# GroupNorm's small products on GpSimd, and the queries' last bias halves behind the first exponentials

## The chip, the core and the metric

The kernel runs on one core of a Trainium2 chip. The metric is the device time of one execution in microseconds (us), the median of several runs. Five engines matter: TensorE (PE in the profile; its weight loads are PEld), VectorE (DVE), ScalarE (ACT), GpSimd (POOL) and the queue that issues the transfers (SP). Each takes its own instructions strictly in order, and they wait for each other by semaphores.

## What is computed

Two attention blocks follow each other, for each of 8 images of 512 channels and 1024 tokens, all in float32:

```python
# layer 0: 32 groups, 8 heads of 64 channels
h   = group_norm(x, gn_weight, gn_bias)
q, k, v = split(w_qkv @ h + b_qkv)                  # per head
a   = softmax((q * s) @ (k * s)) @ v,  s = 64**-0.25
x   = x + w_proj @ a + b_proj
# layer 1: 8 groups, one head of 512 channels
xn  = group_norm(x, gamma, beta)
x   = x + p_w @ (softmax(q1 @ k1 / sqrt(512)) @ v1) + p_b    # q1, k1, v1 from xn
```

A group norm becomes a scale and an offset for each channel: `rstd = (var + eps) ** -0.5`, `s = rstd * weight`, `b = bias - mean * s`. For 512 channels on 128 partitions that is four columns.

## The kernel before

**Products.** Nearly all the work is matrix products on TensorE. The 512 x 512 products are made by Winograd's form of Strassen's scheme, with seven products of half the size in place of eight (`wino`), and the keys and queries of images 1 to 7 apply the scheme twice (`conv2`). Image 0 has its queries and keys from `conv`, with one level.

**conv2.** It works in four `pair`s, numbered `s` = 0 to 3, that hold the outer products (1, 5), (2, 6), (7) and (3, 4). Each pair runs seven inner steps in the order 1, 6, 2, 5, 7, 3, 4. Three pairs of PSUM banks take the sums: bank a for the inner products 1 and 2, b for 6, 7 and 4, c for 5 and 3. ScalarE copies bank a to bank b in step 1 (line 477). In pairs 2 and 3 VectorE adds a bank to what was there before (line 439, in `add`), and TensorE may go on with a bank only when VectorE has read it: step 7 needs bank b after step 6's addition (`u_q`), step 3 needs bank c after step 5's (`c_q`), step 4 needs bank b after step 7's. Pair 2 also sends eight additions of 128x256 to GpSimd (`more`, line 444), which read and write the blocks that pair 3 reads and overwrites. Steps 3 and 4 of a pair, and what is in its list `final`, are put on `tail`, which the next pair runs after its own step 1 (`finish()`).

**The bias of the queries.** `biased_half(i, c)` (line 446) adds it in place with two ScalarE instructions of 128x512 (line 451): for the channel tiles 2i and 2i+1, and the token half c. Half (0, 0) is at the end of pair 1, (1, 1) at the end of pair 2, (0, 1) and (1, 0) at the end of pair 3. The last two thus come just ahead of the attention of that image; its call of `psum_pools` runs what is left on `tail`.

**Attention of layer 0** (`attention0`). Eight stretches for each image: four pairs of heads `hp`, two token halves `tb`. A stretch makes eight tiles of scores (`sc`, two matmuls each), lets ScalarE take the exponential of each (line 590, `e`), sums them on VectorE (lines 592 and 594), and then makes the product with the values (`av`). The tiles of scores rotate through three PSUM pools with one buffer each, so tile n+3 can't start before the exponential of tile n is done. The first stretch reads channel tile 0 and token half 0 of the queries; the second stretch is the first that needs a token half 1. The caller hands in `extra`, sixteen lists of small work: `extra[0]` is run after the first stretch's exponentials have been written down and ahead of its `av`.

**GroupNorm.** `group_mean` and `affine` are two small products with a few small instructions behind. In `affine` (line 123) VectorE reads the variance from PSUM (`ve`, line 126), GpSimd takes the power (`rstd`, line 128), and VectorE makes `s`, `ms` and `b` (lines 130, 132, 134), each of 128x4. There are sixteen of them in a run: two in the prologue, one in the keys of image 1, six behind pair 2 of the queries of images 1 to 6 (line 883, for the next image's layer 0), and seven in layer 1's scores (line 860). The queries of image 7 have none, since no image comes after. `apply` (line 140) uses `s` and `b` on ScalarE; except in the prologue that is a whole stage later.

**What sets the order.** Matmuls are pinned to the order in which the program writes them (`tc.keep_in_program_order`), and so are a few instructions of the other engines. The others are put into their engine's queue by a planner, from its own costs of the instructions and with the order of the program as their priority.

Of the kernel before, what the change touches and what calls it, by code (L numbers as in the profile page):

```python
# [11 lines left out]
AF = mybir.ActivationFunctionType  # L12
ALU = mybir.AluOpType
# [16 lines left out]
def two_attention_blocks_kernel(  # L30
# [8 lines left out]
    nc = tc.nc  # L39
# [26 lines left out]
    def matmul(*args, **kw):  # L66
        tc.keep_in_program_order(nc.tensor.matmul(*args, **kw))  # L67
# [4 lines left out]
    def pcols(name):  # L72
        i = 4 * PARAMS.index(name)
        return par[:, i : i + 4]
# [14 lines left out]
    class GroupNorm:  # L89
# [33 lines left out]
        def affine(self, ps):  # L123
            matmul(ps, gm[:, self.layer, :], self.dv, start=True, stop=True)
            ve = small.tile([P, KC], F32, tag="ve", name=f"ve_{self.uid}")
            nc.vector.tensor_scalar(ve, ps, EPS, None, ALU.add)  # L126
            rstd = small.tile([P, KC], F32, tag="rstd", name=f"rstd_{self.uid}")
            nc.gpsimd.tensor_tensor(rstd, ve, mhalf, ALU.pow)  # L128
            self.s = small.tile([P, KC], F32, tag="s", bufs=4, name=f"s_{self.uid}")
            nc.vector.tensor_mul(self.s, rstd, pcols(f"gn_w{self.layer}"))  # L130
            ms = small.tile([P, KC], F32, tag="ms", name=f"ms_{self.uid}")
            nc.vector.tensor_mul(ms, self.gmean, self.s)
            self.b = small.tile([P, KC], F32, tag="b", bufs=4, name=f"b_{self.uid}")
            nc.vector.tensor_sub(self.b, pcols(f"gn_b{self.layer}"), ms)

        def apply(self, engine, dst, src, c):
            s, b = self.s[:, c : c + 1], self.b[:, c : c + 1]
# [38 lines left out]
    def main_path(ctx):  # L176
# [14 lines left out]
        def acc_tile(name):  # L191
            return ps_acc.tile([P, HT], F32, tag="acc", name=name)
# [5 lines left out]
        def psum_pools(stage, bufs):  # L198
            finish()
            ps_stack.close()  # L200
            ps_pools[:] = [
                ps_stack.enter_context(
                    tc.tile_pool(name=f"ps_{stage}_{n}", bufs=bufs, space=bass.MemoryType.PSUM)
                ) for n in "abc"
            ]

        def load_x(b, c, what):
            t = big_tile(f"{what}_{b}_{c}")
            nc.sync.dma_start(t, x[b, c * P : (c + 1) * P, :])
            return t  # L210
# [12 lines left out]
        def finish():  # L223
            while tail:
                tail.pop(0)()
# [187 lines left out]
                steps.append(make)  # L413
            return f, steps

        def conv2(n, f, bias, name, hooks=()):

# [3 lines left out]
            hooks = list(hooks)  # L423
# [22 lines left out]
            def biased_half(i, c):  # L446
                if bias is not None:
                    for r in range(2):
                        oc = 2 * i + r
                        t = out[oc][:, ts(c, HT)]  # L450
                        nc.scalar.activation(t, t, AF.Identity, bias=bias[:, oc : oc + 1])

            def pair(s, products, y, x, final):
                w = weights2[s // 2][:, (0, 2, 0, 1)[s] :]
# [82 lines left out]
            pair(1, (2, 6), [(0, 0), (0, 1)], [(1, 0), (1, 0)], [load_weight, lambda: biased_half(0, 0)])  # L537
            weights2.append(weight_part((n, 1)))
            pair(2, (7,), [(1, 0)], [(0, 1)], [lambda: biased_half(1, 1)])
            pair(3, (3, 4), [(0, 1), (1, 0)], [(0, 1), (1, 0)], [load_weight, lambda: biased_half(0, 1), lambda: biased_half(1, 0)])  # L540
            return out


# [262 lines left out]
        v, q, k, norm0, later = prologue()  # L806
# [8 lines left out]
        def all_background():  # L815
            run_background(len(background))

        def begun(load, norm, b, what):

            t = [None] * KC  # L820

            def start(c):
                t[c] = load(b, c, what)

            return (
                t, [lambda c=c: start(c) for c in range(KC)],
                [lambda c=c: norm.apply(nc.scalar, t[c], t[c], c) for c in range(KC)],
            )

        def attention_steps(a, scaled, b):  # L830
            af, steps = image_factors(a, f"a_{b}")
            return af, [[], [scaled, lambda: background.extend(steps)]]
# [24 lines left out]
        def norm_hooks(norm, uid):  # L857
            return [
                [], [], [all_background], [lambda: norm.group_mean(acc_tile(f"gmean_{uid}")[:, :KC])],
                [lambda: norm.affine(acc_tile(f"gvar_{uid}")[:, :KC])],  # L860
            ]

        def values(b, h, hooks=()):

            hf, steps = image_factors(h, f"h0_{b}")
            background.extend(steps)
            inner, steps = inner_factors(hf, f"h0_{b}")
            background.extend(steps)
            norm = None
            if b + 1 < B:  # L870
                norm = GroupNorm(0, f"0_{b + 1}")
                for c in range(KC):
                    background.append(lambda c=c: norm.stats(c, load_x(b + 1, c, "ahead")))
            v = by_token(weight("v"), hf, f"v0_{b}", middle=(2, 5, 6, 7), hooks=hooks, back=4, after=[load_weight])
            return v, inner, norm

        def keys_and_queries(b, f, norm, hooks):

            k = conv2("k", f, None, f"k0_{b}", hooks)
            hooks = [[all_background], [], []]  # L880
            if norm:
                hooks[1].append(lambda: norm.group_mean(acc_tile(f"gmean_0_{b + 1}")[:, :KC]))
                hooks[2].append(lambda: norm.affine(acc_tile(f"gvar_0_{b + 1}")[:, :KC]))
            q = conv2("q", f, pcols("bq0"), f"q0_{b}", hooks)
            return q, k

        def layer1_scores(b, h, hooks):
            hf, steps = image_factors(h, f"h1_{b}")
            background.extend(steps)
            g = conv(  # L890
                weight("m"), hf, ubias, f"g1_{b}", middle=(2, 5, 6, 7), hooks=hooks, back=4,
                after=[load_weight, lambda: background.extend(gsteps)],
            )
            stiles = [pair_tile(f"sg{i}_{b}") for i in (1, 2, 4)]
            halves = lambda t: (t[:, :HT], t[:, HT:])
            gf, gsteps = left_sums(
                [halves(t) for t in g[:2]], [halves(t) for t in g[2:]],
                [lambda j, t=t: t[:, j, :] for t in stiles], nc.vector.tensor_add, nc.vector.tensor_sub,
            )
            return hf, gf  # L900
# [22 lines left out]
        for b in range(B):  # L923
            extra = [[] for _ in range(2 * 2 * KC)]
            for i, fs in enumerate(later):
                extra[i] += fs
            later = []
            h, loads, applies = [], [], []
            if b > 0:
                h, loads, applies = begun(load_again, norm1, b - 1, "h1")  # L930
            elif B > 1:
                h, loads, applies = begun(load_x, norm0, 1, "h0")
            for f in loads:
                f()
            for i, f in enumerate(applies):
                extra[2 * i + 3].append(f)
            psum_pools(f"attention_{b}", 1)
            a, scaled = attention0(b, q, k, v, extra)
            psum_pools(f"products_{b}", 2)
            xt = [load_x(b, c, "x") for c in range(KC)]  # L940
            af, ends = attention_steps(a, scaled, b)
            if b > 0:
                hf, gf = layer1_scores(b - 1, h, ends)
                norm1 = projection(b, af, xt)
                if b + 1 < B:
                    h, loads, applies = begun(load_x, norm0, b + 1, "h0")
                else:
                    h, loads, applies = begun(load_again, norm1, b, "h1")
                ahead = [loads, *([f] for f in applies)]
                layer1_rest(b - 1, hf, gf, norm_hooks(norm1, f"1_{b}"), ahead)  # L950
                if b + 1 < B:
                    v, f, norm0 = values(b + 1, h)
                    q, k = keys_and_queries(b + 1, f, norm0, ())
            elif B > 1:
                v, f, norm0 = values(1, h, ends)
                norm1 = projection(0, af, xt)
                q, k = keys_and_queries(1, f, norm0, norm_hooks(norm1, "1_0")[1:])
            else:
                for f in sum(ends, []):
                    f()  # L960
                all_background()
                norm1 = projection(0, af, xt)
                finish()
                for f in sum(norm_hooks(norm1, "1_0"), []):
                    f()
                h, loads, applies = begun(load_again, norm1, 0, "h1")
                for f in loads + applies:
                    f()
# [151 lines left out]
    with ExitStack() as main_ctx:  # L1120
        main_path(main_ctx)
# [45 lines left out]
```

## Time and profile before

| | |
|---|---|
| time, median of 3 runs | 2918.28 us (2915.02 to 2919.66) |
| span of the profiled execution | 2912.7 us |
| PE busy | 2891.4 us (99%) |
| DVE busy | 1940.7 us (67%) |
| ACT busy | 872.3 us (30%) |
| POOL busy | 463.0 us (16%) |
| granted TensorE clock | full in all slices |
| `q` bias, line 451 | 56 instructions, 721 ns in the middle |
| `rstd`, line 128 | 16 instructions, 1017 ns in the middle |
| `s`, line 130 | 16 instructions, 161 to 684 ns, behind 22.2 us of idle VectorE in all |

A row of the groups of instructions gives line, engine, operation, what is written and read (`out<-in`), the shapes, and the count, then the busy time and the mean of one in ns, then the idle time of the engine ahead of it and who ended it. A row of the waits reads: engine, tile and line that waited, whom it waited for, total us, times, longest us. The timeline gives start and duration in us; the same instructions in a row are merged. The page's matmul ends are modelled, so what TensorE loses is best read from the starts of its instructions.

### The profile page before, as it was taken

The numbers are of one execution on the slowest core, as the hardware profiler recorded it, in microseconds if no ns is written. First come the engines' busy times: TensorE is split into PE (matmuls) and PEld (weight loads), VectorE is DVE, ScalarE is ACT, GpSimd is POOL, SyncE is SP. The second block draws the span as 40 slices with busy tenths as digits, with TensorE's granted clock in tenths as the row PEclk, the third lists the DMA queues.
The fourth block names the chain that finished last, engine by engine and source line by source line (L and its number), as shares of the span: only waits on it lengthen the run. The fifth ranks groups of instructions, "written<-read, shape, count | busy, mean of one in ns | idle before, by whom it ended". The sixth has DMA issues, their size and how long they took to land.

```text
span 2912.7 us, 28999 instructions
## 1 busy us (share of the span) xinstructions
PE 2891.4 (99%) x10838; PEld 1495.4 (51%) x10838; DVE 1940.7 (67%) x2661; ACT 872.3 (30%) x1117; POOL 463.0 (16%) x477
## 2 busy tenths in 40 slices
PE   9999999999999999999999999999999999999999
PEld 5436534565345653457434574346733458334544
DVE  5488677566766568665776567866577665776555
ACT  1252451214512055121551115411164112631110
POOL 3023220032100312003210122102111031110000
PEclk9999999999999999999999999999999999999999
DMA  8433303223122231222212232122411223012201
GB/s 276 163 125 119 147 19 116 76 92 131 38 93 91 95 113 48 83 92 108 103 48 80 92 135 77 48 80 95 151 60 44 80 102 141 35 51 73 91 4 66
DMA packets 84186, 267.97 MB, mean 92 GB/s; under 512 B 10371, under 2 KB 29891, under 8 KB 75974
## 3 DMA queue, kind: packets, MB, share of 16 engines
q1 hardware_dynamic: 83622, 265.89, 25.2%
q8 instruction: 87, 1.43, 0.2%
q14 instruction: 61, 0.50, 0.1%
q10 hardware_dynamic: 416, 0.16, 0.0%
HBM read 216.30 MB, written 49.72 MB: 91 GB/s over the span
## 4 chain that ended last, share of the span: by engine, by line
PE 94%; DVE 2%; issue 1%; ACT 1%; POOL 1%; DMA 0%; SPq 0%; DVEq 0%; POOLq 0%; ACTq 0%
PE av L67 15%; PE sc L67 15%; PE psb_sc L67 6%; PE psb_av L67 6%; PE psa_av L67 4%; PE psa_sc L67 4%; PE psc_av L67 4%; PE psc_sc L67 4%; PE psb_z L67 3%; PE psb_p L67 3%; PE psb_g L67 3%; PE psb_v L67 3%; PE psb_k L67 3%; PE psc_z L67 2%; PE psa_z L67 2%; PE psc_p L67 2%
## 5 line engine op out<-in xcount | busy, mean ns | idle before, releaser
L594 DVE TENSOR_TENSOR sum<-sum,e 128x1024 f32<-128x1024 f32 x384 | 518.9, 1351 | 40.4 <-ACT e L590 0.5
L590 ACT ACTIVATE e<-sc 128x1024 f32<-128x1024 f32 x512 | 475.7, 1048 | 63.1 <-PE sc L67 63.1
L67 PE MATMUL sc<-q,k 64*128 64x512 f32 x2048 | 461.8, 598 | 1.1 <-ACT e L590 1.1
L67 PE MATMUL av<-e,v 128*64 128x512 f32 x2048 | 453.6, 595 | 0.0
L67 PEld LDWEIGHTS sc<-q,k 64*128 64x128 f32 x2048 | 188.1, 185 | 248.0 <-ACT e L590 124.0
L67 PEld LDWEIGHTS av<-e,v 128*64 128x64 f32 x2048 | 141.4, 137 | 304.3 <-issue 304.3
L557 POOL TENSOR_TENSOR all_recs<-all_recs,rc 128x256 f32<-128x256 f32 x72 | 64.6, 897 | 896.9 <-DVE rc L555 896.9
L555 DVE RECIPROCAL rc<-sums 128x256 f32<-128x256 f32 x72 | 126.4, 1756 | 88.0 <-PE sums L67 85.7
L611 POOL TENSOR_TENSOR a<-a,r 128x512 f32<-128x512 f32 x56 | 112.1, 2002 | 267.8 <-DMA r<-rows 258.3
L608 ACT COPY a<-av 128x512 f32<-128x512 f32 x64 | 37.5, 586 | 320.9 <-PE av L67 320.9
L642 ACT ACTIVATE e<-e 128x512 f32<-128x512 f32 x96 | 60.5, 630 | 232.6 <-DVE e L641 232.6
L592 DVE TENSOR_TENSOR sum<-e,e 128x1024 f32<-128x1024 f32 x64 | 78.4, 1226 | 66.3 <-ACT e L590 66.3
L67 PE MATMUL psa_sc<-g,h 128*128 128x512 f32 x256 | 115.7, 594 | 0.0
L67 PE MATMUL psa_av<-e,z 128*128 128x512 f32 x256 | 113.3, 595 | 0.0
L140 ACT ACTIVATE h<-h,b,s 128x1024 f32<-128x1024 f32 x62 | 78.6, 1270 | 58.1 <-DMA h<-in_x 46.6
L128 POOL TENSOR_TENSOR rstd<-ve,mhalf 128x4 f32<-128x4 f32 x16 | 16.3, 1018 | 499.9 <-DVE ve L126 499.9
L67 PE MATMUL psb_q<-inner_h,w_q 128*128 128x256 f32 x294 | 75.5, 385 | 6.5 <-DVE u_q L439 6.5
L67 PEld LDWEIGHTS psa_sc<-g,h 128*128 128x128 f32 x256 | 48.1, 190 | 57.9 <-issue 56.2
L67 PEld LDWEIGHTS psa_av<-e,z 128*128 128x128 f32 x256 | 48.0, 190 | 57.3 <-issue 55.4
L67 PE MATMUL psb_k<-inner_h,w_k 128*128 128x256 f32 x294 | 75.3, 383 | 0.0
L249 ACT COPY t_sc<-psa_sc 128x512 f32<-128x512 f32 x32 | 18.7, 586 | 181.7 <-DVE x L843 152.4
L444 POOL TENSOR_TENSOR k<-k,k 128x256 f32<-128x256 f32 x28 | 20.1, 727 | 291.1 <-DVE u_k L439 291.1
(304 smaller groups left out, 4582.9 us busy)
## 6 DMA issues: line engine op xcount, KB each, us to landing
x<-in_x SPq DMA_DIRECT2D x36, 512.0 KB
h<-in_x SPq DMA_DIRECT2D x32, 512.0 KB
r<-rows SPq DMA_DIRECT2D x128, 128.0 KB
spill<-x SPq DMA_DIRECT2D x32, 512.0 KB
h<-spill SPq DMA_DIRECT2D x32, 512.0 KB
x<-spill SPq DMA_DIRECT2D x32, 512.0 KB
out<-x SPq DMA_DIRECT2D x64, 256.0 KB
w_p<-sums_p SPq DMA_DIRECT2D x8, 1792.0 KB
```

Of the source, the lines that this page charges most:

```text
L67: tc.keep_in_program_order(nc.tensor.matmul(*args, **kw))
L140: tc.keep_in_program_order(nc.scalar.activation(dst, src, AF.Identity, bias=b, scale=s))
L249: nc.scalar.copy(t1[i], ps["a", i])
L444: nc.gpsimd.tensor_tensor(d, x, y, ALU.add)
L555: nc.vector.reciprocal(rc, sums)
L557: nc.gpsimd.tensor_tensor(all_recs, all_recs, rc, ALU.add)
L590: nc.scalar.activation(e, sc, AF.Exp, scale=(C // 8) ** -0.5)
L592: nc.vector.tensor_add(total, es[0], e)
L594: nc.vector.tensor_add(total, total, e)
L608: nc.scalar.copy(dst, av)
L611: nc.gpsimd.tensor_tensor(dst, dst, r, ALU.mult)
L642: nc.scalar.activation(dst, dst, AF.Exp, scale=scale)
```

## The change

Two edits, independent of each other.

The first one moves `s`, `ms` and `b` from VectorE to GpSimd, right behind the power that they wait for. VectorE then has no instruction in a norm that waits for GpSimd.

The second one takes the bias halves (0, 1) and (1, 0) of the queries off the end of pair 3 and gives them to the caller in a list, `late`, which is added to `extra[0]` of the attention. They are then queued on ScalarE behind the eight exponentials of the first stretch. All bias instructions of `conv2` are pinned to the program's order.

```diff
@@ affine
-            nc.vector.tensor_mul(self.s, rstd, pcols(f"gn_w{self.layer}"))
+            nc.gpsimd.tensor_tensor(self.s, rstd, pcols(f"gn_w{self.layer}"), ALU.mult)
             ms = small.tile([P, KC], F32, tag="ms", name=f"ms_{self.uid}")
-            nc.vector.tensor_mul(ms, self.gmean, self.s)
+            nc.gpsimd.tensor_tensor(ms, self.gmean, self.s, ALU.mult)
             self.b = small.tile([P, KC], F32, tag="b", bufs=4, name=f"b_{self.uid}")
-            nc.vector.tensor_sub(self.b, pcols(f"gn_b{self.layer}"), ms)
+            nc.gpsimd.tensor_tensor(self.b, pcols(f"gn_b{self.layer}"), ms, ALU.subtract)
@@ conv2
-        def conv2(n, f, bias, name, hooks=()):
+        def conv2(n, f, bias, name, hooks=(), late=None):
...
-                        nc.scalar.activation(t, t, AF.Identity, bias=bias[:, oc : oc + 1])
+                        tc.keep_in_program_order(nc.scalar.activation(t, t, AF.Identity, bias=bias[:, oc : oc + 1]))
...
-            pair(3, (3, 4), [(0, 1), (1, 0)], [(0, 1), (1, 0)], [load_weight, lambda: biased_half(0, 1), lambda: biased_half(1, 0)])
+            last = [lambda: biased_half(0, 1), lambda: biased_half(1, 0)]
+            if late is not None:
+                late += last
+                last = []
+            pair(3, (3, 4), [(0, 1), (1, 0)], [(0, 1), (1, 0)], [load_weight, *last])
@@ keys_and_queries
-            q = conv2("q", f, pcols("bq0"), f"q0_{b}", hooks)
-            return q, k
+            late = []
+            q = conv2("q", f, pcols("bq0"), f"q0_{b}", hooks, late=late)
+            return q, k, late
@@ main loop
+            if b > 0:
+                extra[0] += late
             psum_pools(f"attention_{b}", 1)
...
-                    q, k = keys_and_queries(b + 1, f, norm0, ())
+                    q, k, late = keys_and_queries(b + 1, f, norm0, ())
...
-                q, k = keys_and_queries(1, f, norm0, norm_hooks(norm1, "1_0")[1:])
+                q, k, late = keys_and_queries(1, f, norm0, norm_hooks(norm1, "1_0")[1:])
```

## The prediction

> **What bounds the kernel.** The page first. TensorE is busy for 2891.4 of 2912.7 us and carries 94% of the chain that ended last, so only what lets TensorE start sooner counts. The waits of TensorE name few partners.
>
> ```profile
> PE 2891.4 (99%) x10838; PEld 1495.4 (51%) x10838; DVE 1940.7 (67%) x2661; ACT 872.3 (30%) x1117; POOL 463.0 (16%) x477
> ...
> PE psb_q L67 <- DVE u_q L439: 6.5, 6, 1.1
> ...
> PE psc_q L67 <- DVE c_q L439: 1.2, 6, 0.2
> PE sc L67 <- ACT e L590: 1.1, 7, 0.2
> ```
>
> Six waits in the queries, as many as there are queries with a norm behind pair 2 (images 1 to 6), and seven at scores, as many as there are attentions behind a `conv2`. The ends of matmuls are modelled, so these totals are too small; I take lengths from start to start. The timeline of VectorE in image 1's queries, pair 2 into pair 3, shows the first wait's cause:
>
> ```profile
> 321.30 0.16 DVE L126 TENSOR_SCALAR ve<-gvar 128x4 f32<-128x4 f32 x1 [0.25 <-PE gvar L67]
> 321.38 0.41 DVE L439 TENSOR_TENSOR q<-psb_q,c_q 128x256 f32<-128x256 f32 x1
> 324.37 0.68 DVE L130 TENSOR_TENSOR s<-rstd,par 128x4 f32<-128x4 f32 x1 [2.58 <-POOL rstd L128]
> ...
> 325.37 0.42 DVE L439 TENSOR_TENSOR q<-psc_q,u_q 128x256 f32<-128x256 f32 x1
> 325.70 0.41 DVE L439 TENSOR_TENSOR q<-psb_q,q 128x256 f32<-128x256 f32 x1
> 326.03 0.74 DVE L439 TENSOR_TENSOR u_q<-psb_q,q 128x256 f32<-128x256 f32 x2
> ...
> 323.32 1.02 POOL L128 TENSOR_TENSOR rstd<-ve,mhalf 128x4 f32<-128x4 f32 x1
> 324.31 0.72 POOL L444 TENSOR_TENSOR q<-q 128x256 f32<-128x256 f32 x1
> ...
> 327.35 0.72 POOL L444 TENSOR_TENSOR q<-q 128x256 f32<-128x256 f32 x1
> ```
>
> VectorE stands still for 2.58 us ahead of `s`: the power waits in GpSimd's queue behind four `more` additions and starts at 323.32 though `ve` was there at 321.46. Behind `s` stand the two bank reads of pair 2's steps 3 and 4 and then `u_q`, for which TensorE waits. Image 7's queries have no norm and are the control. The busy times by stretch, from the first matmul of pair 2's step 3 to the first score:
>
> ```profile
> 322.07:330.08 8.01, 6.74 (x30) 4.89 (x28) 5.07 (x15) 2.32 (x4) 5.10 (x7) 1.00 0.72 296
> 2466.26:2472.79 6.53, 6.48 (x31) 4.96 (x29) 4.63 (x12) 2.32 (x4) 4.27 (x7) 1.00 0.90 375
> ```
>
> The first column after the stretch is its length: 8.01 us in image 1, 6.53 in image 7. The norm costs TensorE 1.48 us there.
>
> The second loss, in the same view: a first stretch of attention behind `conv2` (image 1), and the one after it. Then ScalarE's timeline at the start.
>
> ```profile
> 330.08:345.60 15.52, 15.37 (x74) 4.95 (x73) 9.33 (x9) 10.01 (x13) 0.00 (x0) 1.00 0.33 120
> 345.60:360.26 14.66, 14.66 (x78) 5.37 (x74) 11.86 (x9) 9.14 (x11) 2.24 (x2) 1.00 0.05 18
> ...
> 329.78 2.56 ACT L451 ACTIVATE q<-q,par 128x512 f32<-128x512 f32 x4 [0.95 <-DVE q L439]
> 332.24 1.00 ACT L590 ACTIVATE e<-sc 128x1024 f32<-128x1024 f32 x1
> ```
>
> The first stretch takes 15.52 us, a later one 14.66: 0.86 us lost. The four bias instructions hold ScalarE until 332.3, so the first exponential starts 2.16 us after the first score (330.08); in the next stretch it starts 1.17 us after (346.77 against 345.60). The fourth tile of scores needs that exponential's bank and starts at 333.30.
>
> **What the Trainium skill says.** "Perfetto Trace Analysis", Sequencer Loop: an engine instruction waits for its semaphores in its engine's queue; the 2.58 us ahead of `s`, with ready bank reads behind it, agree. "GPSIMD Engine Reference", 3.1: a tensor_tensor of 2048 float32 takes 4497 ns, some 156 ns of it dispatch, hence an estimate of 2.12 ns an element. The trace has 725 ns for 256 elements (line 444) and 2080 ns for 896 (line 306): 2.12 ns an element and 182 ns fixed, which agrees. The same page, 8, warns that GpSimd shares its interfaces with VectorE; for four columns I charge nothing.
>
> **First edit.** It removes from VectorE three instructions of 161 ns and the wait, sixteen times. In images 1 to 6 TensorE gets the 1.48 us that separate it from image 7: 6 x 1.48 = 8.9 us. The other ten: no wait of TensorE's on VectorE over 0.5 us is listed outside the queries, so I count nothing. In layer 1's scores and the keys the stall of VectorE is hidden by matmuls already queued; in the prologue `b` comes some 0.15 us later, and its first user on GpSimd finishes about 23.5, ahead of the first matmul of the values at 25.06.
>
> It adds three 128x4 operations to GpSimd. The trace has none but the power, 1.02 us, an upper bound; the lower is the fixed 0.18. A product isn't a power, and the fixed cost fits two sizes: I take 0.19, with 0.08 between dependent ones as between two `more` (321.88 to 321.95), in all 0.8 us. Queued behind them are four `more` of some 0.7 us. The power ends at 324.34, so they end by 324.34 + 0.8 + 2.9 = 328.0, as they do now (327.35 + 0.72), because two of them wait today for the bank reads that come sooner then. Who waits for the last: VectorE's final additions of pair 3, at 330.25 - 1.48 = 328.8 after the change, and ScalarE's bias (1, 1), whose second instruction would end by 328.8, ahead of the first exponential at about 330.08 - 1.48 + 1.17 = 329.8. Slack 0.8 us and 1.0 us; price nothing. It would be used up at 0.45 us an operation.
>
> **Second edit.** It moves four ScalarE instructions, 2.56 us, to behind the eighth exponential. They end there about 330.08 + 1.17 + 8 x 0.91 + 2.6 = 341.1 on today's clock, hidden by the `av` product, which ends at 345.0; the second stretch needs them then, and ScalarE has 5.5 us of idle time ahead of its copy `a` at 345.14. Behind them on ScalarE stands only that copy. The pins change nothing: ScalarE's order in the trace is the program's already. Of the 0.86 us a part stays: the second tile of scores waits for VectorE's read of bank b (331.00) and starts 1.08 us after the first instead of 0.96, and the third 1.61 instead of 1.39. So 0.22 us stay lost, and 0.64 are won: 7 x 0.64 = 4.5 us. If bank b comes free sooner too, 7 x 0.86 = 6.0.
>
> **Sum.** 8.9 + 4.5 = 13.4 us: 2918.3 - 13.4 = 2904.9.
>
> **Rivals.** (a) Only the first edit pays: at the first stretch the reads of bank b take the place of the exponential as the last wait: 2918.3 - 8.9 = 2909.4. For it: the second tile waits for them already. Against it: that wait is 0.1 us, and the fourth tile loses 0.54. (b) Only the second pays, or GpSimd's queue becomes the bound. At the upper bound, 1.1 us an operation with its gap, the last `more` ends at 324.34 + 3.3 + 2.8 = 330.45, the final addition and the second tile's bank come at 331.2, and the second tile starts 331.35, later than today (331.16); the fourth follows at 333.2 against 333.30. Nearly nothing is won in images 1 to 6, 0.6 us in image 7: about 2917. For it: GpSimd is the chain's link there. Against it: the fixed cost from two sizes. (c) Slower: at 1.5 us an operation the same chain ends 1.2 us later still, so 6 x 1.1 - 0.6 = +6 us: 2924. The planner could also place something else in GpSimd's or VectorE's queue ahead of a bank read, with such a size. Against it: no four-column instruction in the trace is that long, and matmuls are pinned. (d) More than counted: bank b sooner, or the ten other norms worth 0.3 us each, 2900.
>
> **Chances.** Both edits as worked out 0.71, (a) 0.11, (b) 0.08, (c) 0.05, (d) 0.05. The bound of 0.2% is 5.8 us, 2912.4: the main case, (a) and (d) lie below, 0.87; (b) between; (c) above. The runs before spread by 4.6 us, so the range is 2899 to 2912.5: it holds the main case with its 2 us to either side, (a), and most of (d), and leaves out (b) and (c).
>
> **What would show it.** Right: the wait of `psb_q` for `u_q` gone; from pair 2's step 3 to the first score about 6.5 us in images 1 to 6; first stretches of 14.7 to 14.9 us; `s`, `ms`, `b` on GpSimd at about 0.2 us each; the four bias instructions behind eight exponentials; the last `more` ahead of the final addition. Wrong: small operations over 0.45 us, bias (1, 1) waiting for `more` and the exponentials waiting behind it, or a stretch of 8 us that stays.

## The result

The changed kernel takes 2902.52 us (median of 4 runs, 2902.24 to 2905.05), against 2916.65 us for the kernel before in the same comparison: 14.1 us less, a ratio of 0.9953 with a 95% interval of 0.9936 to 0.9970. The forecast was 2904.9 us, within 2899 to 2912.5. The profiled spans, 2912.7 and 2900.9 us, differ by 11.8 us.

The times of most of these kernels fall into two groups, some 3 to 5 us apart (of 33 runs of the kernel before, 18 lie between 2913.2 and 2915.7 us and 15 between 2917.9 and 2921.0), so single steps are read from the starts of TensorE's instructions, and a median only beside them.

### The profile page after: what moved, and what is told of

Its sections match the earlier page's. It is cut to its first block, busy times and chain, and to the rows that moved or that the text cites. A ratio compares the mean times of both kernels' runs of the same rounds, so it can differ in the third digit from the quotient of the medians.

```text
span 2900.9 us, 29024 instructions
## 1 busy us (share of the span) xinstructions
PE 2886.5 (100%) x10838; PEld 1500.3 (52%) x10838; DVE 1932.5 (67%) x2613; ACT 872.2 (30%) x1117; POOL 468.9 (16%) x525
## 3 DMA queue, kind: packets, MB, share of 16 engines
q8 instruction: 87, 1.43, 0.2%
## 4 chain that ended last, share of the span: by engine, by line
PE 98%; issue 1%; DVE 0%; POOL 0%; ACT 0%; DVEq 0%; POOLq 0%
PE sc L67 16%; PE av L67 15%; PE psb_sc L67 6%; PE psb_av L67 6%; PE psa_av L67 4%; PE psa_sc L67 4%; PE psc_av L67 4%; PE psc_sc L67 4%; PE psb_g L67 3%; PE psb_z L67 3%; PE psb_p L67 3%; PE psb_v L67 3%; PE psb_k L67 3%; PE psb_q L67 2%; PE psa_g L67 2%; PE psa_v L67 2%
## 5 line engine op out<-in xcount | busy, mean ns | idle before, releaser
L249 ACT COPY t_sc<-psa_sc 128x512 f32<-128x512 f32 x32 | 18.7, 585 | 181.7 <-DVE x L847 152.4
```

Of the source, the lines that this page charges most:

```text
L249: nc.scalar.copy(t1[i], ps["a", i])
```

## The profile after

TensorE's row of the page, then its waits. (The columns are those of the kernel before. Behind the change in `conv2` the lines of the changed kernel have moved by four: the exponential of line 590 is on line 594.)

```profile
PE 2886.5 (100%) x10838; PEld 1500.3 (52%) x10838; DVE 1932.5 (67%) x2613; ACT 872.2 (30%) x1117; POOL 468.9 (16%) x525
```

```profile
PE psa_v L67 <- POOL h L142: 0.8, 1, 0.8
...
PE psc_q L67 <- DVE c_q L439: 0.4, 1, 0.4
```

The six waits of `psb_q` for `u_q` and the seven of `sc` for `e` are gone. The wait for the normalized image in the prologue, 0.8 us, is new. Of the six waits of `psc_q` for `c_q`, 1.2 us in all before, one of 0.4 us is left, in image 6's queries.

The busy times by stretch for image 1, from pair 2's step 3 to the first score, and the first stretch of attention:

```profile
323.50:330.03 6.53, 6.47 (x30) 4.96 (x28) 4.63 (x12) 1.95 (x3) 5.60 (x10) 1.00 0.88 365
330.03:344.90 14.87, 14.87 (x73) 5.55 (x72) 9.34 (x9) 10.47 (x14) 0.00 (x0) 1.00 0.35 125
```

8.01 has become 6.53 us, and 15.52 has become 14.87. It is so in the other images by the starts of the matmuls: 6.52 to 6.53 us in images 1 to 5 and 6.88 in image 6; 14.88 us in all seven first stretches.

GpSimd's timeline in image 1's queries, and ScalarE's:

```profile
324.75 1.02 POOL L128 TENSOR_TENSOR rstd<-ve,mhalf 128x4 f32<-128x4 f32 x1
325.85 0.20 POOL L130 TENSOR_TENSOR s<-rstd,par 128x4 f32<-128x4 f32 x1
326.00 0.73 POOL L444 TENSOR_TENSOR q<-q 128x256 f32<-128x256 f32 x1
326.69 0.20 POOL L132 TENSOR_TENSOR ms<-gmean,s 128x4 f32<-128x4 f32 x1
326.96 0.20 POOL L134 TENSOR_TENSOR b<-par,ms 128x4 f32<-128x4 f32 x1
...
328.61 0.72 POOL L444 TENSOR_TENSOR q<-q 128x256 f32<-128x256 f32 x1
```

```profile
329.37 0.72 ACT L451 ACTIVATE q<-q,par 128x512 f32<-128x512 f32 x1 [0.77 <-POOL q L444]
331.25 7.55 ACT L594 ACTIVATE e<-sc 128x1024 f32<-128x1024 f32 x8 [1.16 <-PE sc L67]
338.62 2.60 ACT L451 ACTIVATE q<-q,par 128x512 f32<-128x512 f32 x4
```

A product of four columns takes 0.20 us on GpSimd. The last `more` ends at 329.33, ahead of VectorE's final additions at 330.20. Bias (1, 1) ends at 330.09; ScalarE then idles for 1.16 us and takes the first exponential 1.22 us after the first score (330.03). The four late bias instructions end at 341.2, ahead of the copy of `a` at 344.45.

## The experiments

The theory was that two separate waits had been removed: VectorE's for the power (1.48 us in six images) and ScalarE's late first exponential (0.65 us in seven), and that the prologue had lost 1.0 us. The rivals: the two edits need each other; VectorE was relieved of work and not of a wait; GpSimd's queue is far from the path, or close to it.

### The first edit alone

The kernel before with the three lines of `affine` changed.

> The first edit alone; the bias halves stay ahead of the attention. My theory, that VectorE's wait for the power was what cost the queries 1.48 us: the stretch from pair 2's step 3 to the first score falls from 8.01 to about 6.5 us in images 1 to 6, the first stretch of attention stays at 15.5 us, and the prologue loses the 1.0 us that the changed kernel's trace shows ahead of the first product of the values: 8.9 - 1.0 = 7.9 us less than before. Rival, that the two edits need each other (the reads of bank b or GpSimd's queue take over when only one is made): under 4 us.

Measured: 2911.8 us against 2915.66, ratio 0.9982 (0.9976 to 0.9989), 3.9 us less where 7.9 were expected and where the rival had under 4. The lower groups, 2907.6 to 2909.5 and 2913.2 to 2915.7, are about 6 us apart. By TensorE's starts the edit wins 8.6 us in the queries and loses 1.3 in first stretches and 1.0 in the prologue, 6.3 us. The median shows less because 14 of its 21 runs lie in the upper group, and 15 of 33 of the kernel before; the section after next looks at what tells the groups apart. The queries, the first stretch, and ScalarE's timeline:

```profile
326.34:332.86 6.52, 6.46 (x29) 4.96 (x27) 4.62 (x12) 1.93 (x4) 5.61 (x10) 1.00 0.86 358
332.86:348.64 15.78, 15.36 (x73) 4.95 (x72) 9.34 (x10) 10.28 (x14) 0.00 (x0) 1.00 0.33 118
```

```profile
332.22 3.17 ACT L451 ACTIVATE q<-q,par 128x512 f32<-128x512 f32 x5 [0.77 <-POOL q L444]
335.30 1.00 ACT L590 ACTIVATE e<-sc 128x1024 f32<-128x1024 f32 x1
```

The queries gain all they should. The first stretch loses: 15.78 in place of 15.52 us, in images 1 to 5. TensorE comes to the scores 1.48 us sooner, but GpSimd's last `more` does not come sooner, and bias (1, 1) waits for it; five bias instructions now stand in a row ahead of the first exponential, which starts 2.44 us after the first score (332.86) in place of 2.16. So the edits do depend on each other, by 5 x 0.26 = 1.3 us: the first one lets ScalarE's bias instructions run into the attention, and the second one takes four of them out of the way.

### The second edit alone

The changed kernel with the products back on VectorE.

> The second edit alone; s, ms and b stay on VectorE. My theory: the stretch in the queries stays at 8.0 us, the first stretch of attention falls from 15.52 to 14.87 us in images 1 to 7, and the prologue stays as before: 7 x 0.65 = 4.5 us less than before. Rival, that the late bank b is what bounds the first stretch: it stays over 15.3 us and the time within 1.5 us of before.

Measured: 2913.43 us against 2915.66, ratio 0.9988 (0.9979 to 0.9996), 2.2 us less where 4.5 were expected; the lower groups, 2910.0 to 2911.9 and 2913.2 to 2915.7, are 4 us apart.

```profile
327.14:335.15 8.01, 6.73 (x30) 4.88 (x28) 5.07 (x15) 2.01 (x3) 5.11 (x7) 1.00 0.70 292
335.15:350.02 14.87, 14.87 (x73) 5.55 (x72) 9.34 (x9) 10.41 (x13) 0.00 (x0) 1.00 0.33 125
```

The queries stay at 8.01 us, the stretch falls to 14.87. Both halves of the theory hold, each in its own stretch.

### Where the medians fall short: a VectorE instruction of 6 us

The profiles of both single edits have a wait that neither the kernel before nor the changed one shows in its own: `psb_p` for `v`, 2.7 us, in the projection beside image 1's values. Next to it VectorE's timeline has one difference that lasts 6.08 us; in the kernel before the same instruction took 1.24. The clearest profile is that of the experiment on the prologue's norm (its edit is in the next section), VectorE and then GpSimd:

```profile
254.78 6.08 DVE L171 TENSOR_TENSOR t_a<-a 128x512 f32<-128x512 f32 x1
```

```profile
258.18 1.44 POOL L412 TENSOR_TENSOR inner_h<-t_h 128x256 f32<-128x256 f32 x2
259.55 1.89 POOL L412 TENSOR_TENSOR inner_h<-t_h,inner_h 128x256 f32<-128x256 f32 x2
```

GpSimd runs its differences of the second level one behind the other from 252 on. Its first gap, of 78 ns, is the one inside the last row, at 260.30 to 260.38; VectorE's difference ends at 260.86. The suspicion: VectorE's instruction with two operands in SBUF gets no access while GpSimd's queue has no gap. The gap comes where GpSimd reads what its instruction just before has written. The experiment makes such gaps.

```diff
-                        nc.gpsimd.tensor_tensor(dst, x, y, ALU.subtract)
+                        tc.keep_in_program_order(nc.gpsimd.tensor_tensor(dst, x, y, ALU.subtract))
```

This is the changed kernel with the differences of line 411 pinned to the program's order, in which `t2` stands right behind the `t1` that it reads. The planner had interleaved independent ones.

> Both edits, and the differences of the second level (line 411) pinned on GpSimd to the order of the program, in which each t2 stands right behind the t1 that it reads. In some profiles one difference t_a of VectorE, in image 1 ahead of the projection, takes 6.08 us in place of 1.3, while GpSimd runs eight or more differences without a gap; it ends when GpSimd has its first gap of 78 ns. Theory A, that GpSimd's unbroken queue keeps VectorE from the memory: with the gaps of the pinned order no difference of VectorE takes over 2.2 us, the 4 us that separate two groups of times of each kernel are gone, and the times lie together near the lower group of the changed kernel, about 2902. Theory B, that the long one has another cause, for example a transfer: 6 us are seen again and the two groups stay.

Measured: 2904.82 us (2903.84 to 2905.54, 5 runs), ratio 0.9955 (0.9941 to 0.9968). The same instruction:

```profile
257.28 0.93 DVE L170 TENSOR_TENSOR t_a<-a 128x512 f32<-128x512 f32 x1
```

The times lie within 1.7 us of each other, and no VectorE difference in the profile is long. The profiles without the pins agree on the groups: the four that have the long instruction (both single edits, the prologue's norm on VectorE, and the pinned wait further below) are of executions among the upper times of their kernel, 2905.1 to 2914.0 us, and the seven without it, the kernel before and the changed one among them, are of executions among the lower. In the four, TensorE gets from the start of the projection to pair 2 of image 1's queries 3.3 to 5.0 us later than in the seven. So the two groups go with the long instruction, and with the pins neither was seen.

That the gaps did it is not shown. In the changed kernel's profile VectorE's difference, then GpSimd's, at the same place:

```profile
256.37 1.29 DVE L170 TENSOR_TENSOR t_a<-a 128x512 f32<-128x512 f32 x1
256.39 0.72 POOL L411 TENSOR_TENSOR inner_h<-h 128x256 f32<-128x256 f32 x1
257.07 1.85 POOL L411 TENSOR_TENSOR inner_h<-h,inner_h 128x256 f32<-128x256 f32 x2
```

and GpSimd's in the experiment, where VectorE's difference starts at 257.28:

```profile
256.94 0.73 POOL L411 TENSOR_TENSOR inner_h<-h,inner_h 128x256 f32<-128x256 f32 x1
257.64 1.18 POOL L411 TENSOR_TENSOR inner_h<-h 128x256 f32<-128x256 f32 x1
```

In neither is there a gap behind the GpSimd instruction that runs when VectorE's starts (it ends at 257.11 and 257.67, and the next is there at 257.07 and 257.64). VectorE gets its turn there all the same, and the next GpSimd instruction takes 1.17 us in place of 0.72. So VectorE can get in without a gap. The pins also moved the two queues against each other: in all eleven profiles without them the difference starts within 35 ns of a GpSimd instruction's start, in the two with them (the other is that of all mends, below) 0.2 and 0.34 us behind it. Gaps or distance: no run here tells these apart.

Nor is the level that of the changed kernel's lower group, about 2902, as theory A had it: the median is no better. In this profile 1.2 us of it are lost in the first product of layer 1 behind image 5's attention (`psb_g` waits for `u_g`), where VectorE had waited 4.20 us for the transfer of `r`, against 2.98 in the changed kernel's profile. The pins aren't needed for that: the kernel with another bank order, below, has no pins and waits 4.37 us for `r` there, and TensorE 1.5 us. The pins themselves cost 0.09 us at the start of the keys of each of seven images, by TensorE's starts.

### The prologue's norm on VectorE

```diff
+            small_engine = nc.vector if self.pinned else nc.gpsimd
-            nc.gpsimd.tensor_tensor(self.s, rstd, pcols(f"gn_w{self.layer}"), ALU.mult)
+            small_engine.tensor_tensor(self.s, rstd, pcols(f"gn_w{self.layer}"), ALU.mult)
...
```

and likewise for `ms` and `b`; only image 0's first norm is `pinned`.

> Both edits, but the norm of image 0 in the prologue keeps its three products on VectorE. My theory, that GpSimd ends b some 1.2 us later there and TensorE waits for the normalized image: that wait (0.8 us in the changed kernel's trace, 0.97 us from start to start) is gone, and the time is 1.0 us below the changed kernel's, 15 us below before. Rival, that the delay in the prologue is a matter of when the raw weights land in an execution: the gap ahead of the first product of the values stays near 1 us.

Measured: 2901.05 us (2900.02 to 2905.09), 0.9949 (0.9936 to 0.9963), 14.6 us below before where 15 were expected. The three lower runs, 2900.0 to 2901.1, lie 1.2 to 2.6 us below the changed kernel's three, 2902.2 to 2902.7. TensorE's timeline at the start of the values, first in the changed kernel, then here:

```profile
24.17 1.45 PE L67 MATMUL ps_wm<-natk,natq 128*128 128x512 f32 x3
26.41 0.45 PE L67 MATMUL psa_v<-prepare_v,h 128*128 128x256 f32 x1 [0.80 <-POOL h L142]
```

```profile
23.60 1.45 PE L67 MATMUL ps_wm<-natk,natq 128*128 128x512 f32 x3
24.89 0.59 PE L67 MATMUL psa_v<-prepare_v,h 128*128 128x256 f32 x2
```

From the first of three matmuls to the values: 2.24 us there, 1.29 here, as in the kernel before (23.77 to 25.06). The change costs 0.95 us in the prologue.

### VectorE held back in the prologue

Why does `b` come so late there? GpSimd's timeline of the changed kernel in the prologue:

```profile
20.64 1.42 POOL L128 TENSOR_TENSOR rstd<-ve,mhalf 128x4 f32<-128x4 f32 x1 [19.13 <-DVE ve L126]
22.14 0.42 POOL L130 TENSOR_TENSOR s<-rstd,par 128x4 f32<-128x4 f32 x1
22.64 0.52 POOL L132 TENSOR_TENSOR ms<-gmean,s 128x4 f32<-128x4 f32 x1
23.24 0.20 POOL L134 TENSOR_TENSOR b<-par,ms 128x4 f32<-128x4 f32 x1
```

All but `b` are longer than elsewhere. VectorE, which no longer waits, sums the weights at the same time (20.48 to 23.11). The experiment makes it wait again, by one copy of `b` that it has to make first:

```diff
                 norm.affine(acc_tile("gvar_0_0")[:, :KC])
+                held = small.tile([P, KC], F32, tag="held", bufs=1, name="held")
+                tc.keep_in_program_order(nc.vector.tensor_copy(held, norm.b))
```

> Both edits, and in the prologue one small copy of b on VectorE that holds its weight sums back until b is there, as they were held before. Theory A, that GpSimd's small instructions there were stretched by VectorE's sums of two inputs at the same time: power 1.02 us and 0.20 us for each product in the prologue, in place of 1.42, 0.42 and 0.52, b about 0.9 us sooner, and TensorE's wait for the normalized image gone or under 0.2 us. Theory B, that they were long because they are the first of their kind on GpSimd: 1.4, 0.4 and 0.5 us stay and the wait stays near 0.8 us.

```profile
21.04 1.03 POOL L128 TENSOR_TENSOR rstd<-ve,mhalf 128x4 f32<-128x4 f32 x1 [19.52 <-DVE ve L126]
22.15 0.20 POOL L130 TENSOR_TENSOR s<-rstd,par 128x4 f32<-128x4 f32 x1
22.43 0.20 POOL L132 TENSOR_TENSOR ms<-gmean,s 128x4 f32<-128x4 f32 x1
```

1.03 and 0.20 us: theory A. TensorE's wait is gone. The five times, 2900.4 to 2905.74 us with a median of 2904.38, spread too far to show a gain of 1 us.

### How much slack GpSimd's queue has

Both edits, with `ms` written nine times in the six norms of the queries.

```diff
-            nc.gpsimd.tensor_tensor(ms, self.gmean, self.s, ALU.mult)
+            for _ in range(self.times):
+                nc.gpsimd.tensor_tensor(ms, self.gmean, self.s, ALU.mult)
```

> Both edits, and ms written nine times in place of once in the norms behind pair 2 of the queries, images 1 to 6: eight more small operations on GpSimd, 8 x 0.28 = 2.2 us in its queue (the result is the same). It measures the slack that the prediction put at 0.8 us. My theory: the last addition of GpSimd ends 2.2 us later, 1.4 us after VectorE's final additions want it, and TensorE's second tile of scores comes about 1.4 us later in six images: 8 us above the changed kernel, about 2911. Rival, that GpSimd's queue is not near the path (the planner puts the additions first, or other slack is left): within 1 us of the changed kernel.

Measured: 2908.98 us (2907.44 to 2913.45), 0.9972 (0.9966 to 0.9979), by the ratios some 5.5 us above the changed kernel where 8 were expected. The nine take 2.42 us, and the last `more` now ends at 331.29. TensorE, in image 1:

```profile
329.89 1.13 PE L67 MATMUL sc<-q,k 64*128 64x512 f32 x4
331.90 1.56 PE L67 MATMUL sc<-q,k 64*128 64x512 f32 x6 [0.88 <-DVE q L441]
```

The second tile of scores waits for VectorE's final additions, as the prediction's rival (b) has it. The loss from start to start is 0.91 us in images 1 to 5 and 0.56 in image 6, 5.1 us in all. Of 2.2 us more work 1.3 were free: 0.87 of slack, as above, and the rest because only the second of the two final additions waits for the last `more` (the first starts at 330.53).

### The 0.2 us that stay

```diff
-                        sc = ps_pools[n % 3].tile([P, 2, HT], F32, tag="sc", name=f"sc_{uid}_{s}")
+                        sc = ps_pools[(0, 2, 1)[n % 3]].tile([P, 2, HT], F32, tag="sc", name=f"sc_{uid}_{s}")
```

> Both edits, and the tiles of scores rotate through the PSUM pools in the order a, c, b in place of a, b, c, so that the second tile takes bank c, which is read 0.9 us earlier than bank b. My theory, that the 0.2 us left of the loss in a first stretch are the wait for the read of bank b: first stretches of 14.66 us in place of 14.87, 7 x 0.21 = 1.5 us below the changed kernel. Rival, that they come with ScalarE's first exponential or the change of matmul shape: 14.87 stays.

```profile
330.06:344.71 14.65, 14.65 (x73) 5.31 (x73) 9.33 (x9) 10.37 (x14) 0.00 (x0) 1.00 0.35 127
```

14.65 us in all seven first stretches, what a later stretch takes. The 0.22 us were the read of bank b. The median, 2906.09 us (2902.75 to 2907.76; ratio 0.9959, 0.9946 to 0.9972), doesn't show the 1.6 us. In its profile, of the fastest of the five runs, `psb_g` waits for `u_g` for 1.5 us as above; what held up the four others isn't known.

### The wait without the move

The second edit, with `s`, `ms` and `b` on VectorE as before, but those of the queries' norms written down behind the late bias halves. First without a pin (`late.append(norm.products)`):

> The second edit, and the products s, ms, b all stay on VectorE, but those of the six norms in the queries are written down only behind the late bias halves, in the attention. VectorE has the same instructions as before, only not in front of the bank reads. My theory, that the wait in VectorE's queue was the cost and not the work or its engine: the stretch in the queries is 6.5 us in images 1 to 6 as in the changed kernel, the prologue is as before, and the time is about 1 us below the changed kernel's. Rival, that VectorE needed the relief: the stretch stays above 7 us.

Measured: 2913.68 us, 0.9988 (0.9981 to 0.9994). It tested nothing, as VectorE's timeline shows:

```profile
324.43 0.69 DVE L137 TENSOR_TENSOR s<-rstd,par 128x4 f32<-128x4 f32 x1 [2.58 <-POOL rstd L129]
```

The planner put them where they had been. With the first one pinned (`tc.keep_in_program_order(first)`):

> As e8_wait_only, but the first of the late products is pinned behind what VectorE already has at that place in the program. In e8 the planner had put them back in front of the bank reads (s at 324.43, 2.59 us after the power's operand), so nothing had been tried. Now VectorE does the same work as before, in the attention, without a wait. My theory, that the wait ahead of the bank reads was the cost: the stretch in the queries is 6.5 us in images 1 to 6 and the time is about 1 us below the changed kernel's, since the prologue is as before. Rival, that it was VectorE's work that had to go: the stretch stays over 7 us and the time near 2910.

```profile
326.51:333.04 6.53, 6.47 (x30) 4.96 (x29) 4.62 (x12) 2.01 (x3) 5.08 (x7) 1.00 0.88 366
```

6.53 us, and in image 6 also 6.52, with VectorE's work unchanged (`s` now at 345.45, 0.15 us, without idle time ahead). So it was the products' place in front of the bank reads, where they wait for the power, and not VectorE's work as a whole or its engine. The time is 2904.69 us (2901.29 to 2905.79), 0.9958 (0.9944 to 0.9971), 2.0 us above the changed kernel beside it (next section) and not 1 us below as was expected. Its profile has the 6.07 us instruction; the prologue's 0.95 us are won.

### All mends together

The prologue's products on VectorE, the pools in the order a, c, b, and the pins on line 411; beside it the changed kernel again.

> Both edits with three mends: the prologue's products on VectorE, the order a, c, b of the pools for the scores, and GpSimd's differences pinned to the order of the program. If the three causes are apart: 1.0 us from the prologue, 1.5 us from seven first stretches, and no 6 us difference on VectorE in any execution, so a median near 2900, 2 to 4 us below the changed kernel in the same call, with times that lie within 3 us. Rival, that the mends give back what they win (the pins delay GpSimd, the earlier TensorE waits elsewhere): equal to the changed kernel, 2902 to 2905.

> The changed kernel once more, unaltered, beside its mended form. The long difference in image 1 is a matter of how two engines' instructions meet, so its times should fall in two groups 4 us apart like those of before: near 2902 and near 2905 to 2906, median 2902 to 2905.

Measured side by side: 2901.36 us (2900.67 to 2901.64) with the mends, ratio to before 0.9950 (0.9936 to 0.9963); 2902.69 us (2902.15 to 2907.95), 0.9959 (0.9945 to 0.9972), for the changed kernel. The gain over the changed kernel is 1.3 us by the medians, less than the 2 to 4 expected, and within the two intervals. What is clear is the spread: 1.0 us against 5.8 (four of the changed kernel's five runs lie between 2902.15 and 2903.33, the fifth at 2907.95).

```profile
PE psb_g L67 <- DVE u_g L239: 1.2, 2, 1.0
```

Against the changed kernel's profile beside it, by TensorE's starts, it wins 0.95 us in the prologue, 1.6 in the stretches (7 x 0.23) and 0.35 in image 6's queries. It loses 1.0 more in this wait, 0.4 at projections and 0.6 at the starts of the keys (7 x 0.09), which only the two profiles with the pins lose. So the rival holds in part: the mends give back more than half of what they win.

## Why the prediction was right

**First edit, the queries: right.** 1.48 us were named from image 7 as the control, and images 1 to 5 won 1.49 each. Image 6 won 1.14: its step 3 waits 0.4 us for `c_q`, which no step foresaw. The products on GpSimd don't make that wait by themselves: it is absent with the prologue's norm on VectorE or VectorE held back there, where the queries' products stay on GpSimd. Why it comes, and in image 6 alone, is open. In all 8.6 us for 8.9.

One reading was wrong: "three instructions of 161 ns". In the six norms of the queries `s` takes 0.68 us, and ends 0.02 us or less behind the `more` that GpSimd has begun just before it (in image 1, 324.31 to 325.03 against 324.37 to 325.05). So 1.0 us of the products themselves (324.37 to 325.37), and not their wait alone, stood ahead of the bank reads. The control by image 7 holds both, so the sum didn't suffer.

**GpSimd's queue: right, with a better measure.** 0.19 us for a product, measured 0.20. The slack to the final additions was put at 0.8 us and is 0.87 (329.33 to 330.20), to the first exponential at 1.0 and is 1.16. With 2.2 us more in the queue, rival (b)'s chain came about: the second tile of scores waited for the final additions. The end of the last `more` is 1.26 us later by the clock than before, not the same, because the prologue and the start of the execution shifted everything by 1.43 us; relative to TensorE it is as worked out.

**Second edit: right.** 0.64 us a stretch, measured 0.65: 4.5 us. The 0.22 us that were to stay did, and they are the read of bank b, as named. (The 1.61 and 1.39 us given there for the third tile are those of the second tile's last matmul; the third starts 2.01 us after the first, against 1.82 in a later stretch.)

**The prologue: wrong, and small.** The step was "in the prologue `b` comes some 0.15 us later" and its first user finishes well ahead of the matmul. It came 1.2 us later, of which 0.9 are the longer power and products, and TensorE waited 0.95 us. The sentence behind it was also wrong: "for four columns I charge nothing" for the shared interface. "SBUF — State Buffer" in the Trainium skill, SBUF: two separate sides, says that a VectorE instruction with two SBUF inputs and a GpSimd instruction that reads SBUF contend for one pair of ports: the one that starts first holds it for the whole instruction, and the other is blocked. The traces agree that they hold each other up, with 1.42 us for 1.03 and 0.52 for 0.20. The price came from what the freed VectorE does next: with VectorE held back the power takes 1.03 us and each product 0.20.

**What the sum left out.** The terms measured by TensorE's starts, 8.6 + 4.5 - 0.95 = 12.1 us, fit the profiled spans' 11.8, with 0.4 us lost to the start of that execution; 13.4 were forecast. The timed 14.1 us has an interval from 8.7 to 18.7, in which both lie, and its excess over 12.1 fits the mix of the two groups, two and two runs before, three and one after. That the timed gain came out above the forecast, and not below it as the prologue's loss would have it, is luck of that mix. Edits were summed as if independent, and the change is described so; they aren't (the first alone loses 1.3 us in the first stretches), but made together each wins in its own stretches what the sum gave it, but for image 6.

Rival (a) was ruled out by the fourth tile, which no longer waits; (b) was a matter of price, and (c) with it. Of (d) nothing came: bank b came no sooner relative to the scores, and from one image's queries to the next TensorE wins 2.1 us (357.3 to 355.2 between images 1 and 2), which is 1.49 + 0.65 and leaves nothing for the other norms.

## What to carry to other kernels

Find out what stands behind a waiting instruction in its engine's queue before asking what the instruction costs: three products, 1.0 us with what GpSimd's work beside them added, held up TensorE for 1.48 us, because they waited for another engine ahead of bank reads. If the same program has a place without the piece of work, as image 7 here, its length is the price: here to the hundredth in five images of six. And when an engine is freed of a wait, look at what it starts sooner and with whom that shares its way to the memory.

## What was not expected of the hardware

A VectorE difference of 128x512 with both operands in SBUF lasted 6.04 to 6.08 us in four of the thirteen profiles, in place of 0.7 to 1.3. In these four GpSimd ran eight two-operand instructions without a gap meanwhile, and the difference ended half a microsecond after the first gap of 78 ns. In the other nine the same difference got its turn when the one GpSimd instruction that was running ended, though the next stood behind it without a gap. So GpSimd and VectorE don't always take turns, and which of them goes on when both have an instruction waiting changes from one execution to the next of the same program. What settles it is open.

The long instruction costs TensorE 3.3 to 5.0 us here and goes with the upper of the two groups of times. The page named above says that the ports are held for a whole instruction; the nine profiles agree, and the four show more than that, a VectorE instruction passed over at seven ends of GpSimd instructions in a row. Dependent instructions of GpSimd leave a gap of 78 ns each; with them placed right behind each other the long instruction was not seen in two profiles and ten runs, but whether because of the gaps stays open, as said above.
